# Graph network layer on one core: the first nodes and node numbers of the sums' one-hot matrices kept in PSUM

## The chip, the core and the metric

The kernel runs on one core of a Trainium2 chip. A core has TensorE (matrix products, which are written to PSUM), VectorE (DVE) and ScalarE (ACT) for elementwise work, GpSimd (POOL), which here issues the gathers, SyncE (SP), which issues the plain DMAs, and 16 DMA engines. SBUF is the working memory and PSUM the memory of 8 banks that the products land in; both have 128 partitions. The metric is the device time of one execution in microseconds (us); a kernel's time is the median over its runs.

## What is computed

The input is 6250 nodes with 512 features each and 100,000 edges (src, dst), sorted by dst. Cut to what matters:

```python
norm = -dinv[src] * dinv[dst]            # dinv = 1/sqrt(out-degree), 0 where there is none
def prop(h):                             # weighted sum over the incoming edges of each node
    return segment_sum(h[src] * norm[:, None], dst, num_segments=6250)
def conv(h, W0, W1, b):
    return h @ W0 + prop(h) @ W1 + b

h = maximum(layernorm(x), 0)
h = conv(h, W1_0, W1_1, b1)              # layer 1
h = layer_norm(h, gamma, beta)
h = where(h >= 0, h, 0.01 * h)
out = x + conv(h, W2_0, W2_1, b2)        # layer 2
```

All is in fp32. The heavy part is `prop`: for each of the 100,000 edges a row of 512 floats is fetched by its src and added to the row of its dst, once in each of the two layers.

## The kernel before

**Setup.** The kernel loads the edge list and x, counts the out-degrees with one-hot matmuls, takes the layer norm's statistics, and writes a table `tab` of rows already scaled by dinv, from which the first layer gathers. The edges are cut into NC = 782 chunks of 128, one edge on each partition. Transposed by TensorE, the chunks' source nodes become columns of `sidx`, and their destination nodes (plus one) columns of `dlx`; both stay in SBUF.

**Units and groups of the sums.** Three chunks (STEP) make a unit. A unit's sums cover a span of Q = 32 successive nodes, which begins at the node of the unit's first edge; four units (NQ) make a group and fill the 128 partitions of one PSUM tile. There are NS = 66 groups in a layer. The first node of every unit is found in the setup: the matmul of line 320 puts the last row of selected columns of `dlx` on all 128 partitions, in the PSUM tile `first_ps` of 265 columns, and line 321 copies that into `first` in SBUF.

**Gathers.** `gather_to` (line 379) issues one indirect DMA per chunk on GpSimd (line 382): 128 rows of 2 KB, picked by a column of `sidx`, into one of the 57 `places` in SBUF. Each layer has 782; the first 60 of layer 1 read x itself and 16 of those are issued early, on line 212. A place is used again when the matmuls of an earlier group have read it.

**Sums.** `sums(g)` (line 461) makes the one-hot matrices on VectorE and the sums on TensorE. Line 465 adds 1 to 32 to each of the group's four first nodes and so writes `node`, 128x128, a tile with two buffers. Line 474 compares the destination nodes of the group's chunks (`dlx`, read with broadcasts) with `node`, and so writes `sel`, 128x512, also with two buffers: a 1 stands where an edge of a partition belongs to a node of the span. Line 480 multiplies the 32 columns of `sel` of a chunk and a unit with the gathered rows; four chunks (SPAN) go into each unit, up to 16 products in a group, all into one `ps`. Line 483 copies `ps` to SBUF as `agg`.

**Blocks.** The nodes are also cut into 49 blocks of 128. When the groups that can hold a block's nodes are summed, `turn` transposes the block's own rows (`own`), and `place` moves its sums from the groups' spans to the block's rows by further one-hot products (`there`, line 493; matmul, line 496). `dense` multiplies both with the weights (line 458), and `finish` adds the bias and, in layer 1, takes layer norm, scales and stores the rows into the second layer's table `tab[1]` and into `h_tab`; in layer 2 it adds x and stores the result.

**Order.** TensorE, GpSimd and SyncE keep the order in which the program is written (a manual schedule); for VectorE and ScalarE a scheduler orders instructions by readiness and places the semaphores. In each group GpSimd is given the next 12 gathers first, then come the blocks that are due, the sums, and the dense products. In layer 1 there are also, in the opening, the tables that are still to be scaled (`make_table`, lines 393 to 397) and the look-up of scales for the rows gathered straight from x (`find` and `look_up`, lines 403 to 434). The second layer's first gather waits for the last row stored into `tab[1]`.

**PSUM.** In the loops the pool `main_ps` holds `ps`, `hT_ps` and `u_ps` with two buffers each and `aT_ps` with one: seven of the eight banks.

Of the kernel before, what the change touches and what calls it, by code (L numbers as in the profile page):

```python
# [8 lines left out]
F32 = mybir.dt.float32  # L9
# [10 lines left out]
P = 128  # L20
# [4 lines left out]
Q = 32  # L25
NQ = P // Q
# [13 lines left out]
def gnn_kernel(  # L40
# [33 lines left out]
    nc = tc.nc  # L74
    N, D = x.shape
# [10 lines left out]
    NS = -(-NU // NQ)  # L86
# [10 lines left out]
    tab = [dram.tile([n, D], F32, name=f"tab{i}") for i, n in enumerate((NB * P, N))]  # L97
    h_tab = dram.tile([N, D], F32, name="h_tab")
    ndinv_d = dram.tile([NB * P], F32, name="ndinv_d")

    ident = const.tile([P, P], F32, name="ident")
    iota_r = const.tile([P, P], F32, name="iota_r")
    ones = const.tile([P, P], F32, name="ones")
    eps = const.tile([P, 1], F32, name="eps")
# [5 lines left out]
    dlx = const.tile([P, 1 + STEP * NQ * NS + 1], F32, name="dlx")  # L110
    first = const.tile([P, NQ * NS + 1], F32, name="first")
    node_of = const.tile([P, NS], F32, name="node_of")
    minus = const.tile([P, 1], F32, name="minus")
# [5 lines left out]
    sidx = const.tile([P, NG * P], I32, name="sidx")  # L119
    w_sb = [const.tile([P, KD, D], F32, name=f"w{i}") for i in range(2)]  # L120
# [9 lines left out]
    stay = ExitStack()  # L130
# [2 lines left out]
    order = list(range(NB, NB + RE)) + list(range(w_at))  # L133
    w_late = places[:, w_at:NB, :].rearrange("p (i k) d -> p i k d", i=2)

    edges = ctx.enter_context(ExitStack())
    ep = edges.enter_context(tc.tile_pool(name="edges", bufs=1))
    src_i = ep.tile([EP, EJ], I32, name="src_i")
# [24 lines left out]
    while i < NB:  # L163
        n = min(NB - i, (2, 6, 8)[len(groups)] if len(groups) < 3 else 7)
# [37 lines left out]
    with tc.tile_pool(name="turn", bufs=1) as wp, tc.tile_pool(  # L202
        name="turn_ps", bufs=2, space=bass.MemoryType.PSUM
# [7 lines left out]
    for t in range(RE):  # L211
        nc.gpsimd.indirect_dma_start(
            out=places[:, order[t], :], out_offset=None, in_=x,
# [7 lines left out]
    for (i0, n), t in zip(groups, xs):  # L221
        n = min(n, NB - LAST - i0)
# [13 lines left out]
    with tc.tile_pool(name="deg", bufs=1) as dp, tc.tile_pool(name="onehot", bufs=2) as ohp, tc.tile_pool(  # L236
        name="deg_ps", bufs=1, space=bass.MemoryType.PSUM
# [37 lines left out]
    with tc.tile_pool(name="fold", bufs=1) as dp, tc.tile_pool(  # L275
        name="fold_ps", bufs=1, space=bass.MemoryType.PSUM
# [27 lines left out]
    with tc.tile_pool(name="turn", bufs=1) as wp, tc.tile_pool(  # L304
        name="turn_ps", bufs=1, space=bass.MemoryType.PSUM
    ) as wps:
        f = wp.tile([P, NG, P], F32, name="f")
        nc.vector.tensor_scalar_add(f, chunks[1], 1.0)
        dl_ps = wps.tile([P, NG * P], F32, name="dl_ps")
        for g in range(NG):  # L310
            nc.tensor.transpose(dl_ps[:, g * P : (g + 1) * P], f[:, g, :], ident)
        nc.scalar.activation(dlx[:, 1 : 1 + NC], dl_ps[:, :NC], AF.Copy)
        down = wp.tile([P, NG, P - 1], F32, name="down")
        nc.vector.tensor_tensor(down, f[:, :, 1:], f[:, :, : P - 1], op=OP.is_lt)
        nc.vector.tensor_reduce(unsorted, down.rearrange("p g e -> p (g e)"), AX.X, OP.add)


        last = ident[:, P - 1 : P]
        first_ps = wps.tile([P, NQ * NS + 1], F32, name="first_ps")
        nc.tensor.matmul(first_ps, last.to_broadcast([P, P]), dlx[:, 0 : STEP * NQ * NS + 1 : STEP], start=True, stop=True)  # L320
        nc.vector.tensor_copy(first, first_ps)
        row_ps = wps.tile([P, 2, NS], F32, name="row_ps")
        for k in range(2):
            for q in range(NQ):
                at = STEP * (q + k)
                nc.tensor.matmul(row_ps[q * Q : (q + 1) * Q, k, :], last.to_broadcast([P, Q]),
                                 dlx[:, at : at + STEP * NQ * (NS - 1) + 1 : STEP * NQ], start=True, stop=True)
        p_i = ep.tile([P, 1], I32, name="p_i")
        p_j = ep.tile([P, 1], F32, name="p_j")
        held = ep.tile([P, NS], F32, name="held")  # L330
        nc.vector.tensor_copy(p_i, p_id)
        nc.vector.tensor_single_scalar(p_i, p_i, Q - 1, op=OP.bitwise_and)
        nc.vector.tensor_copy(p_j, p_i)
        nc.vector.tensor_scalar(node_of, row_ps[:, 0, :], p_j, 1.0, op0=OP.add, op1=OP.add)
        nc.vector.tensor_tensor(held, row_ps[:, 1, :], node_of, op=OP.is_ge)
        nc.vector.tensor_mul(node_of, node_of, held)
        nc.vector.tensor_scalar_mul(minus, last, -1.0)
        rows_ps = wps.tile([NB, P], F32, name="rows_ps")
        nc.tensor.transpose(rows_ps, ndinv, ident)
        rows_sb = ep.tile([NB, P], F32, name="rows_sb")  # L340
        nc.scalar.activation(rows_sb, rows_ps, AF.Copy)
        nc.sync.dma_start(ndinv_d.rearrange("(b p) -> b p", p=P), rows_sb)

    edges.close()
    unseen = const.tile([1, 1], I32, name="unseen")
    usual_path(tc, locals())
    stay.close()
    n_unseen = nc.values_load(unseen[0:1, 0:1], min_val=0, max_val=1,
# [5 lines left out]

def usual_path(tc, have):
    nc = tc.nc
    (x, out, tab, h_tab, ndinv_d, sidx, dlx, iota_r, w_sb, W2_1, W2_0, w_late, ident, eps, ones, first, node_of, minus,
     unsorted, ln, dinv, sdinv, bias1, bias2, gam, bet, unseen, N, E, D, NB, NC, NU, NS, KD, rows, places, order,
     groups, xs, sc, pick, src_lo, src_hi, p_id, dup) = (
        have[n] for n in ("x out tab h_tab ndinv_d sidx dlx iota_r w_sb W2_1 W2_0 w_late ident eps ones first node_of "  # L360
                          "minus unsorted ln dinv sdinv bias1 bias2 gam bet unseen N E D NB NC NU NS KD rows places "
                          "order groups xs sc pick src_lo src_hi p_id dup").split())
    AHEAD = 2
# [5 lines left out]
    with ExitStack() as es:  # L369
        pool = es.enter_context(tc.tile_pool(name="main", bufs=2))  # L370
# [5 lines left out]
        def zr(t):  # L376
            return places[:, order[t % R], :]
# [83 lines left out]
        def sums(g):  # L461

            n = min(NQ, NU - NQ * g)
            node = pool.tile([P, NQ, Q], F32, name="node")
            nc.vector.tensor_tensor(node[:, :n, :], first[:, NQ * g : NQ * g + n, None].to_broadcast([P, n, Q]),
                                    iota_r[:, None, 1 : Q + 1].to_broadcast([P, n, Q]), op=OP.add)
            sel = pool.tile([P, NQ, SPAN, Q], F32, name="sel")
            chunk = [range(STEP * (NQ * g + q), min(STEP * (NQ * g + q) + SPAN, NC)) for q in range(n)]
            same = n if len(chunk[-1]) == SPAN else 1
            for q in range(0, n, same):  # L470
                w = len(chunk[q])
                of = dlx[:, 1 + chunk[q][0] : 2 + chunk[q][0]]
                of = bass.AP(tensor=of.tensor, offset=of.offset, ap=[of.ap[0], [STEP, same], [1, w], [0, Q]])
                nc.vector.tensor_tensor(sel[:, q : q + same, :w, :], of,  # L474
                                        node[:, q : q + same, None, :].to_broadcast([P, same, w, Q]), op=OP.is_equal)
            ps = psum.tile([P, D], F32, name="ps")
            for s in range(SPAN):
                for q in range(n):
                    if s < len(chunk[q]):
                        nc.tensor.matmul(ps[q * Q : (q + 1) * Q, :], sel[:, q, s, :], zr(chunk[q][s]), start=(s == 0),  # L480
                                         stop=(s == len(chunk[q]) - 1))
            agg[g] = pool.tile([P, D], F32, name="agg", bufs=4)
            nc.scalar.activation(agg[g][: n * Q], ps[: n * Q], AF.Copy)  # L483
# [134 lines left out]
        for layer in range(2):  # L618
# [5 lines left out]
            for g in range(NS):  # L624
# [13 lines left out]
                while inside[i].stop <= g:  # L638
                    due.append((i, turn(layer, i)))
                    i += 1  # L640
                sums(g)
                if layer == 0:
                    if g == 0:
# [344 lines left out]
```

## Time and profile before

| | us |
|---|---|
| median of 3 runs | 2149.52 |
| lowest and highest run | 2146.58, 2150.33 |
| the profiled execution | 2148.89 |
| its span, first to last instruction | 2146.7 |
| GpSimd busy, 1577 instructions | 1520.2 |
| TensorE busy with products | 1795.7 |
| VectorE busy | 674.8 |
| mean granted TensorE clock | 0.926 of full speed |

The profile is one execution, taken by the hardware profiler. Its lines are read like this. "L382 POOL DMA_INDIRECT places<-tab,sidx x1504 | 1444.5, 960 | 493.8 <-issue 315.8" says that line 382 of the kernel ran 1504 times on GpSimd, writing `places` from `tab` by the indices in `sidx`; 1444.5 us in all, 960 ns on average; before these instructions the engine was idle for 493.8 us, and most of that (315.8 us) ended with nothing that the profile shows ("issue"). PEld is TensorE's loading of weights, PE its products. In the row of 40 slices each digit is the busy share of a fortieth of the span, in tenths. A line of waits names the waiting engine, tile and line, then what it waited for, the sum in us, how often, and the longest one. A line of the timeline gives start and duration in us, engine, line, operation, the tiles written and read with their shapes, and in square brackets the idle time before it and what ended that.

### The profile page before, as it was taken

How to read it: one execution, taken by the hardware profiler on the slowest of the kernel's cores; microseconds unless marked ns; L12 is line 12 of the kernel's file. 1: busy time of each engine (PE TensorE's matmuls, PEld its weight loads, DVE VectorE, ACT ScalarE, POOL GpSimd, SP SyncE). 2: the span in 40 equal slices, each digit the busy share in tenths (PEclk: the TensorE clock that was granted, in tenths of full speed). 3: DMA queues.
4: the chain of work that ended last, by engine and by line, in shares of the span. 5: the costliest groups of instructions: out<-in, count | busy, mean ns of one | idle time of the engine just before them, and what ended most of it. 6: DMA issues, size and time to landing. Idle time of an engine off the chain costs nothing.

```text
span 2146.7 us, 23527 instructions
## 1 busy us (share of the span) xinstructions
PE 1795.7 (84%) x8843; PEld 794.7 (37%) x8843; DVE 674.8 (31%) x1341; ACT 382.7 (18%) x694; POOL 1520.2 (71%) x1577
## 2 busy tenths in 40 slices
PE   5669888988879888988876888889888888889888
PEld 4534333333334333433331333334333333334333
DVE  8974323333334233333330212212212212211211
ACT  7774212111112122111110000000000000000000
POOL 5067777777777777777727777777777777777772
PEclk9779999999989999999997989999999999999989
DMA  9298888788788888788837788888878888877883
GB/s 368 82 354 264 247 254 254 242 250 255 243 286 249 253 255 250 240 255 244 254 121 229 243 251 256 255 251 245 256 243 255 243 251 257 256 248 247 245 252 117
DMA packets 198945, 527.05 MB, mean 246 GB/s; under 512 B 31864, under 2 KB 46019, under 8 KB 198822
## 3 DMA queue, kind: packets, MB, share of 16 engines
q0 software_dynamic: 125120, 410.09, 62.4%
q1 hardware_dynamic: 73702, 115.36, 15.5%
q8 instruction: 71, 1.16, 0.2%
q14 instruction: 52, 0.43, 0.1%
HBM read 474.06 MB, written 51.27 MB: 245 GB/s over the span
## 4 chain that ended last, share of the span: by engine, by line
PE 48%; DMA 29%; POOL 9%; issue 8%; DVE 5%; ACT 0%; POOLq 0%; SPq 0%; ACTq 0%; DVEq 0%
DMA places<-tab,sidx 28%; PE u_ps L458 25%; PE ps L480 15%; POOL places L382 9%; PE aT_ps L496 5%; PE hT_ps L451 1%; DVE hi L252 1%; DVE lo L252 1%; DVE places L393 0%; PE both_ps L258 0%; DMA places<-in_x_dram,sidx 0%; DVE places L394 0%; PE u_ps L422 0%; PE hT_ps L422 0%; DVE both L428 0%
## 5 line engine op out<-in xcount | busy, mean ns | idle before, releaser
L382 POOL DMA_INDIRECT places<-tab,sidx x1504 | 1444.5, 960 | 493.8 <-issue 315.8
L480 PE MATMUL ps<-places,sel 128*32 128x512 f32 x4168 | 732.4, 666 | 280.7 <-DMA places<-tab,sidx 268.1
L480 PEld LDWEIGHTS ps<-places,sel 128*32 128x32 f32 x4168 | 141.8, 117 | 781.0 <-DMA places<-tab,sidx 591.3
L474 DVE TENSOR_TENSOR sel<-dlx,node 128x512 f32<-128x512 f32 x132 | 90.9, 688 | 750.0 <-PE ps L480 750.0
L496 PE MATMUL aT_ps<-there,agg 128*128 128x128 f32 (+2 forms) x2080 | 253.8, 278 | 1.4 <-ACT agg L483 1.4
L496 PEld LDWEIGHTS aT_ps<-there,agg 128*128 128x128 f32 (+1 forms) x2080 | 246.1, 196 | 4.2 <-ACT agg L483 3.2
L483 ACT ACTIVATE agg<-ps 128x512 f32<-128x512 f32 x132 | 78.8, 597 | 918.9 <-PE ps L480 918.9
L458 PE MATMUL u_ps<-places,hT 128*128 128x512 f32 (+1 forms) x392 | 185.8, 618 | 0.7 <-ACT hT L453 0.7
L458 PE MATMUL u_ps<-w,hT 128*128 128x512 f32 (+1 forms) x392 | 181.1, 605 | 0.7 <-ACT hT L453 0.7
L458 PE MATMUL u_ps<-places,aT 128*128 128x512 f32 (+1 forms) x392 | 178.0, 597 | 0.7 <-DVE aT L548 0.7
L458 PE MATMUL u_ps<-w,aT 128*128 128x512 f32 (+1 forms) x392 | 176.3, 592 | 0.7 <-DVE aT L548 0.7
L506 DVE TENSOR_TENSOR u_ps<-u_ps,bias 128x512 f32<-128x512 f32 x48 | 33.6, 700 | 294.9 <-PE u_ps L458 294.9
L511 DVE TENSOR_TENSOR u_ps<-u_ps,bias 128x512 f32<-128x512 f32 (+1 forms) x49 | 34.3, 700 | 284.3 <-PE u_ps L458 284.3
L453 ACT ACTIVATE hT<-hT_ps 128x512 f32<-128x512 f32 (+1 forms) x98 | 58.3, 595 | 349.6 <-PE hT_ps L451 348.2
L458 PEld LDWEIGHTS u_ps<-places,hT 128*128 128x128 f32 (+1 forms) x392 | 72.3, 195 | 117.3 <-issue 116.5
L458 PEld LDWEIGHTS u_ps<-w,hT 128*128 128x128 f32 (+1 forms) x392 | 70.3, 189 | 109.0 <-issue 106.5
L458 PEld LDWEIGHTS u_ps<-places,aT 128*128 128x128 f32 (+1 forms) x392 | 74.8, 191 | 95.4 <-issue 94.6
L458 PEld LDWEIGHTS u_ps<-w,aT 128*128 128x128 f32 (+1 forms) x392 | 74.3, 190 | 94.3 <-issue 93.4
L382 POOL DMA_INDIRECT places<-in_x_dram,sidx x44 | 45.0, 1024 | 86.8 <-ACT places L396 57.7
L448 ACT ACTIVATE h<-h,ln 128x512 f32<-128x512 f32 (+1 forms) x49 | 39.7, 813 | 283.3 <-DMA h<-in_x_dram 283.3
L493 DVE TENSOR_SCALAR there<-iota_r,node_of 128x128 f32<-128x128 f32 x260 | 76.6, 295 | 38.7 <-PE aT_ps L496 38.6
L548 DVE TENSOR_TENSOR aT<-aT_ps,to 128x512 f32<-128x512 f32 (+1 forms) x98 | 67.1, 685 | 39.4 <-PE aT_ps L496 37.9
(128 smaller groups left out, 942.7 us busy)
## 6 DMA issues: line engine op xcount, KB each, us to landing
places<-tab,sidx POOLq DMA_INDIRECT x1504
h<-in_x_dram SPq DMA_DIRECT2D x48, 256.0 KB
tab<-t SPq DMA_DIRECT2D x48, 256.0 KB
h_tab<-g SPq DMA_DIRECT2D x48, 256.0 KB
h<-h_tab SPq DMA_DIRECT2D x48, 256.0 KB
xt<-in_x_dram SPq DMA_DIRECT2D x48, 256.0 KB
out_dram<-t SPq DMA_DIRECT2D x48, 256.0 KB
places<-in_x_dram SPq DMA_DIRECT2D x4, 1792.0 KB
```

The source lines that it names most:

```text
L252: nc.vector.tensor_tensor(t, s[:, g * 2 * GJ : (g + 1) * 2 * GJ].rearrange("p (j s) -> p j s", s=2)[:, :, None, :] .to_broadcast([EP, GJ, ...
L382: nc.gpsimd.indirect_dma_start(out=zr(t), out_offset=None, in_=x if layer == 0 and t < RAW else tab[layer], in_offset=bass.IndirectOffsetO ...
L448: nc.scalar.activation(h[:r], h[:r], AF.Relu, bias=ln[:r, 1, i : i + 1], scale=ln[:r, 0, i : i + 1])
L453: nc.scalar.activation(hT[:, :, :r], ps[:, :, :r], AF.Copy)
L458: nc.tensor.matmul(u_ps[:r], hT[:, kc, :r], w[:, kc, :], start=(start and kc == 0), stop=(not start and kc == KD - 1))
L474: nc.vector.tensor_tensor(sel[:, q : q + same, :w, :], of, node[:, q : q + same, None, :].to_broadcast([P, same, w, Q]), op=OP.is_equal)
L480: nc.tensor.matmul(ps[q * Q : (q + 1) * Q, :], sel[:, q, s, :], zr(chunk[q][s]), start=(s == 0), stop=(s == len(chunk[q]) - 1))
L483: nc.scalar.activation(agg[g][: n * Q], ps[: n * Q], AF.Copy)
L493: nc.vector.tensor_scalar(there[:m, :r], iota_r[:m, :r], node_of[:m, g : g + 1], -(1.0 + i * P), op0=OP.subtract, op1=OP.is_equal)
L496: nc.tensor.matmul(placed[i][:, kc, :r], agg[g][:m, kc * P : (kc + 1) * P], there[:m, :r], start=(g == inside[i][0] and kc == 0), stop=(g ...
L511: nc.vector.tensor_add(v, v, bias1[:r])
L548: nc.vector.tensor_tensor(aT[:, :, :r], placed.pop(i)[:, :, :r], to.pop(i)[:, None, :r].to_broadcast([P, KD, r]), op=OP.mult)
```

## The change

The first nodes of the units no longer live in a tile of the setup's PSUM pool, but in a PSUM bank of their own, `nodes_ps`, which stays through both layers; the copy into `first` in SBUF is kept, since the final check reads it. The group's node numbers `node` are no longer an SBUF tile with two buffers, but the last 128 columns of the same bank, written anew for each group. So line 465 reads the first nodes from PSUM and writes PSUM, and line 474 reads `dlx` from SBUF and `node` from PSUM. No instruction is added or left out. `nodes_ps` takes the bank that `main_ps` leaves free.

```diff
@@ gnn_kernel
     w_late = places[:, w_at:NB, :].rearrange("p (i k) d -> p i k d", i=2)
 
+    nodes_ps = stay.enter_context(tc.tile_pool(name="nodes_ps", bufs=1, space=bass.MemoryType.PSUM)).tile(
+        [P, D], F32, name="nodes_ps")
+    assert NQ * NS + 1 <= D - P
     edges = ctx.enter_context(ExitStack())
...
         last = ident[:, P - 1 : P]
-        first_ps = wps.tile([P, NQ * NS + 1], F32, name="first_ps")
+        first_ps = nodes_ps[:, : NQ * NS + 1]
         nc.tensor.matmul(first_ps, last.to_broadcast([P, P]), dlx[:, 0 : STEP * NQ * NS + 1 : STEP], start=True, stop=True)
         nc.vector.tensor_copy(first, first_ps)
@@ usual_path: nodes_ps is handed over; then in sums(g)
             n = min(NQ, NU - NQ * g)
-            node = pool.tile([P, NQ, Q], F32, name="node")
-            nc.vector.tensor_tensor(node[:, :n, :], first[:, NQ * g : NQ * g + n, None].to_broadcast([P, n, Q]),
+
+            node = nodes_ps[:, D - P :].rearrange("p (q e) -> p q e", q=NQ)
+            nc.vector.tensor_tensor(node[:, :n, :], nodes_ps[:, NQ * g : NQ * g + n, None].to_broadcast([P, n, Q]),
                                     iota_r[:, None, 1 : Q + 1].to_broadcast([P, n, Q]), op=OP.add)
             sel = pool.tile([P, NQ, SPAN, Q], F32, name="sel")
```

More of the change, by code (lines that the diff above doesn't have):

```diff
@@ L356, in usual_path @@
     nc = tc.nc
-    (x, out, tab, h_tab, ndinv_d, sidx, dlx, iota_r, w_sb, W2_1, W2_0, w_late, ident, eps, ones, first, node_of, minus,
+    (x, out, tab, h_tab, ndinv_d, sidx, dlx, iota_r, w_sb, W2_1, W2_0, w_late, ident, eps, ones, first, nodes_ps, node_of, minus,
      unsorted, ln, dinv, sdinv, bias1, bias2, gam, bet, unseen, N, E, D, NB, NC, NU, NS, KD, rows, places, order,
      groups, xs, sc, pick, src_lo, src_hi, p_id, dup) = (
-        have[n] for n in ("x out tab h_tab ndinv_d sidx dlx iota_r w_sb W2_1 W2_0 w_late ident eps ones first node_of "
+        have[n] for n in ("x out tab h_tab ndinv_d sidx dlx iota_r w_sb W2_1 W2_0 w_late ident eps ones first nodes_ps node_of "
                           "minus unsorted ln dinv sdinv bias1 bias2 gam bet unseen N E D NB NC NU NS KD rows places "
```

## The prediction

> **What bounds the kernel now.** I read first the busy line, then the GpSimd row of the 40 slices, then the groups, then the waits of GpSimd and of the matmul engine, and last the timeline around single gathers.
>
> ```profile
> PE 1795.7 (84%) x8843; PEld 794.7 (37%) x8843; DVE 674.8 (31%) x1341; ACT 382.7 (18%) x694; POOL 1520.2 (71%) x1577
> POOL 5067777777777777777727777777777777777772
> ...
> L382 POOL DMA_INDIRECT places<-tab,sidx x1504 | 1444.5, 960 | 493.8 <-issue 315.8
> L474 DVE TENSOR_TENSOR sel<-dlx,node 128x512 f32<-128x512 f32 x132 | 90.9, 688 | 750.0 <-PE ps L480 750.0
> ```
>
> TensorE has the largest busy share, yet it is not what sets the pace. GpSimd's row is a flat 7 from the fourth slice to the end with one dip in the middle: a gather takes 0.95 us, and the next starts 0.30 us after it. A flat 7 is therefore an engine that always has its next gather ready, at 1.254 us a gather. The waits say the same from both sides:
>
> ```profile
> POOL places L382 <- issue: 320.7, 1052, 0.3
> POOL places L382 <- DMA tab<-t: 35.1, 1, 35.1
> POOL places L382 <- PE ps L480: 30.3, 98, 0.8
> ...
> PE ps L480 <- DMA places<-tab,sidx: 268.1, 198, 14.0
> PE ps L480 <- DVE sel L474: 10.0, 2, 8.1
> ```
>
> The last column is the longest single wait. GpSimd's waits for a freed place (PE ps) are the ordinary 0.3 us step between gathers; one is 0.8 us. The one real stop is the 35.1 us between the layers, when the second layer's first gather waits for the table that the first has finished. The matmuls wait 268.1 us for rows that have not landed, spread over both layers: in every full 100 us from 200 to 2100 TensorE sits idle 7.8 to 34 us. They wait for sel only twice, in the opening. So from about 126 us to the last gather at 2109.7 us time is the number of gathers times their pitch, plus the 35.1 us stop, plus whatever lengthens single gathers.
>
> Something does lengthen them. The gathers' median is 0.949 us, the mean 0.960, the longest 1.46. Two places in the timeline, Vector rows and GpSimd rows:
>
> ```profile
> 865.83 0.69 DVE L474 TENSOR_TENSOR sel<-dlx,node 128x512 f32<-128x512 f32 x1 [13.84 <-PE ps L480]
> 865.95 1.40 POOL L382 DMA_INDIRECT places<-tab,sidx  x1 [0.30 <-PE ps L480]
> 867.65 0.95 POOL L382 DMA_INDIRECT places<-tab,sidx  x1 [0.30 <-issue]
> ...
> 842.72 0.76 DVE L521 SCALAR_TENSOR_TENSOR u_ps<-u_ps,rs,bet 128x512 f32<-128x512 f32 x1
> 843.11 0.95 POOL L382 DMA_INDIRECT places<-tab,sidx  x1 [0.30 <-issue]
> ```
>
> The comparison L474 started 0.12 us before the gather at 865.95 and ended 0.57 us after the gather's start; the gather took 1.40 us, 0.45 too much. At 843.11 L521, with its data in PSUM, lay across a gather's start in the same way, and the gather took its 0.95. Over the whole trace the pattern is exact: where L474 runs from before a gather's start to more than 0.13 us after it, the gather is longer than 0.949 us by (end of L474 - start of gather - 0.13 us). From 126 us on, L474 lies so (0.15 us or more past the start) across 67 gathers and lengthens 61; L465, which also reads two SBUF tiles (first and iota_r), 7 of 11. Instructions that read one operand from PSUM and at most one wide operand from SBUF (L428, L506, L507, L511, L514, L519, L521, L525, L530, L548) lie so across 199 and lengthen none.
>
> **The change, part by part.** Nothing is added or removed: GpSimd and ScalarE have the same instructions in the same order, TensorE and VectorE the same number.
>
> *The lock on the gathers.* L474 reads dlx from SBUF and node from PSUM; L465 reads first from PSUM and iota_r from SBUF. Each has one SBUF input left. Summing each lengthened gather's excess over 0.949 us by the instruction whose end it follows: L474 10.70 us in layer 1 (36 gathers) and 7.00 us in layer 2 (25); L465 0.43 + 0.16 us and 0.25 us (8). Together 18.5 us. The page's rows check the size: 1444.5 - 1504 x 0.949 = 17.2 us for the gathers from tab, where 18.1 of my 18.5 us lie (the rest of the difference is gathers of 0.942 to 0.948). It is also what chance would give. An L474 of 0.693 us that starts at a random point of a 1.254 us pitch hits if it starts in the 0.563 us that end at the gather's start, with a mean excess of 0.28 us: 0.45 x 0.28 x 132 = 16.7 us.
>
> [...] I take 18.5 us; the other end is 0.
>
> *What stays locked.* L393 and L394 (2.6 us of excess before 145 us) and L425 (0.5 us) are untouched. L493 lengthened 4 gathers, 0.18 us in all. Its position relative to the gathers shifts; at random, 257 of 0.28 us would cost 257 x 0.12 x 0.075 = 2.3 us. Ends: 0 to 2.1 us more than now; I take 0.5, near the row, since its instructions follow the same TensorE work as before.
>
> *Duration of the two Vector instructions.* No row has L474's new pair (first input SBUF, second PSUM). [...] The nearest rows say none: L548, PSUM and SBUF to SBUF at the same size, takes 0.685, L507 0.691 against L474's 0.688; L506 and L511, which read and write one PSUM bank as L465 will, 0.700. I take 0.00 to 0.01 us each. Either way it costs no end time: VectorE is busy 31%, and sel is made a group ahead (two buffers, written when the sums two groups back are done), so some 15 us of other matmuls cover it. [...]
>
> *One buffer for node in place of two.* node of the next group must now follow sel of this one. In steady order it did already (at 866.56 L465 follows L474 at once). In the opening a few instructions change places: before, two L465 stand together ahead of the third L474; now each L465 follows its L474, so one node of 0.29 us moves. Behind it on VectorE is that L474, and TensorE waits for it. That is the only place where TensorE waits for sel (10.0 us), and GpSimd already runs ahead there: 0 to 0.3 us, taken as 0.
>
> *The PSUM bank.* The loops' seven banks and this one fill PSUM; the setup matmul L320 and copy L321 stay, one writing elsewhere. Cost 0; bounds -0.3 to +0.5 us, if some setup tile waits one matmul group for a shared bank.
>
> *What is late next.* Gathers land some 2.9 us after their issue ends, the same at the start and the end of a layer, so the DMA engines are not backed up at 81% busy; 1% more rate is absorbed. TensorE's slack, 7.8 us or more in each 100 us, stands against 0 to 1.6 us of savings in the same stretches, so it keeps up. The 35.1 us stop and the some 36 us after the last gather are chains of TensorE and Vector work that keep their length.
>
> **Sum.** 18.5 - 0.5 = 18.0 us off. The profiled execution took 2148.9 us (span 2146.7 and 2.2 around it): 2130.9. The median of the runs, 2149.5, is 0.6 above that execution, so I forecast 2131.5 us, 0.84% less.
>
> **The rivals.**
> - *Given back in part.* TensorE, or the chain at the layers' ends, takes over where blocks follow closely (a group with a block holds some 14.4 us of matmuls in a 15.05 us group), or L493 begins to hit. For: a margin of 0.6 us in those groups. Against: the idle time in every stretch. Half given back: 2140.
> - *No change.* The lock is not from two SBUF inputs but from something L474 keeps (dlx from SBUF as the first input, or the write to SBUF). For: no row has an SBUF first input beside a PSUM one. Against: L548 writes the same shape to SBUF across 40 gather starts without effect. 2149.5.
> - *Slower.* VectorE's single node buffer makes sel late: L465 queued behind an L474 that waits for the sums, TensorE stops at L480, and then the places come free late for GpSimd. Its place is every group, its point the 15 us by which sel is ahead; each us past it costs 132 us. An L474 of 0.76 us (the longest now) and an L465 of 0.36 are far below. Only if the PSUM reads took several us each would it decide; 2 us lost in a tenth of the groups gives 2149.5 - 18 + 26 = 2158.
>
> **How the numbers follow.** Full gain 0.82, in part 0.08, no change 0.05, slower 0.05. The likeliest gives 2131.5, its own range 2127 to 2137: the 18.5 us whole with a run at the low end of the three shown (2.9 below the median) up to L493 at random and 3 us at the layers' ends. For 8 in 10 with the partly lost cases, 2127 to 2141. What a measurement here can tell is about 0.2%, 4.3 us. Faster takes the first two cases, 0.90; same 0.05; slower 0.05.
>
> **What would show it.** Right: the gathers' mean falls from 0.960 to about 0.951 with the same 0.30 us step, no gather after 150 us over about 1.1 us, the longest ones beside L493; L474 and L465 within 0.02 us of now; the waits of GpSimd unchanged, the stop still about 35 us. Wrong: gathers still ending 0.82 us after an L474 does; GpSimd waiting for PE ps by more than a few us (TensorE bound); TensorE waiting for sel in mid-run.

## The result, and the profile after

The changed kernel takes 2127.65 us (median of 6 runs, 2126.33 to 2129.85). The kernel before, run beside it, takes 2145.54 us (median of 6, three of which are the runs shown above). The ratio is 0.9911, 95% interval 0.9898 to 0.9924: 19 us less by the ratio, 17.9 by the two medians. The forecast was 18.0 us less and 2131.5 us, its own range 2127 to 2137. The saving came as forecast; the absolute time came out 3.85 us under the forecast, at the lower edge of the range. The term that was off is the time from which the saving was taken, not the saving.

The page of the changed kernel (profiled execution 2129.0 us; its line numbers are 3 or 4 higher, so that L382, L474 and L493 of before are L385, L478 and L497):

```profile
span 2127.2 us, 23561 instructions
...
PE 1786.6 (84%) x8843; PEld 793.0 (37%) x8843; DVE 678.2 (32%) x1341; ACT 382.0 (18%) x694; POOL 1496.7 (70%) x1577
...
POOL 5057777777777777777727777777777777777772
...
L385 POOL DMA_INDIRECT places<-tab,sidx x1504 | 1422.6, 946 | 492.9 <-issue 313.8
L478 DVE TENSOR_TENSOR sel<-dlx,nodes_ps 128x512 f32<-128x512 f32 x132 | 89.8, 680 | 726.5 <-PE ps L484 726.4
```

GpSimd is busy 23.5 us less (1520.2 to 1496.7) and the span is 19.5 us shorter; its idle time before the gathers is the same (493.8 and 492.9), and its row is the same flat 7. VectorE is busy 3.4 us more. So the time left the gathers. The waits of GpSimd, and the two waits of TensorE that were to be watched, in the same columns as before:

```profile
POOL places L385 <- issue: 318.9, 1047, 0.3
...
POOL places L385 <- DMA tab<-t: 35.0, 1, 35.0
POOL places L385 <- PE ps L484: 21.0, 69, 0.3
...
PE ps L484 <- DMA places<-tab,sidx: 256.0, 174, 14.3
...
PE ps L484 <- DVE sel L478: 10.1, 2, 8.2
```

No wait took the place of the lock: GpSimd never waits longer than its step of 0.3 us for a place that the sums free, the stop between the layers kept its 35 us, TensorE still waits 256 us for rows, and for sel only the same two times in the opening.

Two views of the changed kernel's trace. The first is the row of its gathers from `tab`, with the shortest, median and longest duration in ns and the first and last start in us. The others show one comparison that lies across a gather's start:

```profile
L385 POOL DMA_INDIRECT places<-tab,sidx x1504: 942/946/1062, 174.1 to 2088.4; - x188
...
899.29 0.69 DVE L478 TENSOR_TENSOR sel<-dlx,nodes_ps 128x512 f32<-128x512 f32 x1 [4.70 <-PE ps L484]
...
899.53 0.95 POOL L385 DMA_INDIRECT places<-tab,sidx  x1 [0.30 <-issue]
```

The longest gather from tab is 1.06 us where it was 1.46. At 899.53 the comparison began 0.24 us ahead of the gather and ended 0.45 us into it; in the first trace of before the 11 comparisons that ended 0.43 to 0.47 us into a gather cost it 0.30 to 0.34 us, here it cost nothing. Over the trace the comparison lies across 69 gather starts (0.15 us or more past the start, from 125 us on) and lengthens none; the addition L469 lies across 10 and lengthens none.

### The profile page after: what moved, and what is told of

Same layout as the page of the kernel before. It is cut to its first block, busy times and chain, and to the rows that moved or that the text cites. A ratio compares the mean times of both kernels' runs of the same rounds, so it can differ in the third digit from the quotient of the medians.

```text
span 2127.2 us, 23561 instructions
## 1 busy us (share of the span) xinstructions
PE 1786.6 (84%) x8843; PEld 793.0 (37%) x8843; DVE 678.2 (32%) x1341; ACT 382.0 (18%) x694; POOL 1496.7 (70%) x1577
## 3 DMA queue, kind: packets, MB, share of 16 engines
q8 instruction: 71, 1.16, 0.2%
## 4 chain that ended last, share of the span: by engine, by line
PE 35%; DMA 32%; POOL 15%; issue 12%; DVE 4%; ACT 1%; POOLq 0%; SPq 0%; ACTq 0%; DVEq 0%
DMA places<-tab,sidx 32%; PE u_ps L461 16%; POOL places L385 15%; PE ps L484 13%; PE aT_ps L500 4%; PE hT_ps L454 1%; DVE hi L255 1%; DVE lo L255 1%; PE both_ps L261 1%; PE hT_ps L425 0%; DVE places L396 0%; ACT places L436 0%; DVE places L397 0%; PE u_ps L425 0%; DMA src_c<-in_src_dram 0%
## 5 line engine op out<-in xcount | busy, mean ns | idle before, releaser
L385 POOL DMA_INDIRECT places<-tab,sidx x1504 | 1422.6, 946 | 492.9 <-issue 313.8
L478 DVE TENSOR_TENSOR sel<-dlx,nodes_ps 128x512 f32<-128x512 f32 x132 | 89.8, 680 | 726.5 <-PE ps L484 726.4
L385 POOL DMA_INDIRECT places<-in_x_dram,sidx x44 | 43.5, 989 | 89.8 <-ACT places L399 58.8
L497 DVE TENSOR_SCALAR there<-iota_r,node_of 128x128 f32<-128x128 f32 x260 | 79.7, 307 | 43.3 <-PE aT_ps L500 41.4
```

What stands on the lines that cost most here:

```text
L385: nc.gpsimd.indirect_dma_start(out=zr(t), out_offset=None, in_=x if layer == 0 and t < RAW else tab[layer], in_offset=bass.IndirectOffsetO ...
L478: nc.vector.tensor_tensor(sel[:, q : q + same, :w, :], of, node[:, q : q + same, None, :].to_broadcast([P, same, w, Q]), op=OP.is_equal)
L497: nc.vector.tensor_scalar(there[:m, :r], iota_r[:m, :r], node_of[:m, g : g + 1], -(1.0 + i * P), op0=OP.subtract, op1=OP.is_equal)
```

## The experiments

Two theories stood against each other. *Lock:* a Vector instruction with two SBUF inputs that is running when a gather starts holds the gather up until it ends, and GpSimd's pace is the kernel's. (A gather that is held up is called hit.) *Rivals:* the time on VectorE counts, or where things lie in PSUM, or the gathers as such became shorter (their median was 949 ns in the first profile of before and 946 in that of after). In what follows "lengthened" means longer than 0.965 us, the excess is counted over the mean of the others in the same trace, and all is from 130 us on, after the opening.

### The kernel before again, and the changed one beside it

No edit. Both were profiled on the same chip.

> The kernel before, unchanged, profiled on the same chip as the runs beside it. Two profiles of different executions showed gathers of 0.949 us (before) and 0.946 us (after) in the median; 3 ns over 1548 gathers are 4.6 us. If that difference belongs to the execution or the chip and not to the change, this profile shows the same median as the changed kernel's profile of the same chip (within 1 ns), and the whole saving between the two spans is that of the lengthened gathers, some 17 to 18.5 us. If it belongs to the change, this one shows 0.949 again and the changed one 0.946. Ratio to itself 1.000 within 0.002. Lengthened gathers behind the comparison of 128x512: some 60, 16 to 19 us.

> The changed kernel, unchanged, on the same chip. Lock theory: ratio 0.9915 (18 us less) and no gather lengthened behind the two instructions that now read PSUM; the rival that the gathers as such became shorter: 0.9895 to 0.991, with the gathers' median 3 ns under that of the kernel before in the profile of this chip.

Measured: the kernel before 2149.7 us, ratio to its other runs 1.0005 (0.9995 to 1.0016); the changed one 2130.33 us, ratio 0.991 (0.9892 to 0.9927). The gathers of before, a comparison with the gather that it met, and then the gathers of the changed kernel:

```profile
L382 POOL DMA_INDIRECT places<-tab,sidx x1504: 942/949/1457, 172.8 to 2115.1; - x188
...
1251.32 0.69 DVE L474 TENSOR_TENSOR sel<-dlx,node 128x512 f32<-128x512 f32 x1 [3.69 <-PE ps L480]
...
1251.65 1.19 POOL L382 DMA_INDIRECT places<-tab,sidx  x1 [0.30 <-issue]
```

```profile
L385 POOL DMA_INDIRECT places<-tab,sidx x1504: 942/949/1023, 172.1 to 2093.1; - x188
```

Both have a median of 949 here: the changed kernel's 946 in its first profile was that execution's. So the gathers as such did not become shorter by the change; they have two levels (below). The ratio alone could not have said so: 0.991 is the edge of what that rival expected, and its interval holds the lock theory's 0.9915 as well. Lengthened: 90 gathers with 26.1 us before; 10 with 0.7 us after, none of them behind the two instructions that now read PSUM, which lay across 75 and 18 starts. The lock theory's 16 to 19 us behind the comparison was too low for this execution of before, which had 78 of them with 24.5 us and was the slowest of its ten runs (2156.69 us). How many gathers the comparison hits differs between executions of one kernel: 61 in the first trace of before, 78 in this one.

### The comparison alone

```diff
-            nc.vector.tensor_tensor(node[:, :n, :], nodes_ps[:, NQ * g : NQ * g + n, None].to_broadcast([P, n, Q]),
+            nc.vector.tensor_tensor(node[:, :n, :], first[:, NQ * g : NQ * g + n, None].to_broadcast([P, n, Q]),
```

This is an edit to the changed kernel: node stays in PSUM, the first nodes come from SBUF.

> The node numbers stand in PSUM and the comparison reads them there, as in the change; but the first nodes are read from SBUF, so the small addition (128x128) still has two SBUF inputs. Lock theory: of the 18.5 us the comparison's share, 17.7, is gained and the addition's 0.8 is not (between 0.3 and 3 us of lengthened gathers behind it, since its place relative to the gathers moves): ratio 0.9915 to 0.993. If both had to be in PSUM, or if it is the first nodes' place that counts, 0.998 to 1.000.

Measured: 2129.15 us, ratio 0.9906 (0.989 to 0.9921), 2.6 us of lengthened gathers. Behind the comparison none (65 starts), behind the addition with its two SBUF inputs 11 with 0.67 us. The gain is the comparison's; the addition's share is too small for the timing, but its gathers show it. The ratio lies just under the expected band, whose 0.9915 the interval holds.

### The addition alone

```diff
-            node = nodes_ps[:, D - P :].rearrange("p (q e) -> p q e", q=NQ)
+            node = pool.tile([P, NQ, Q], F32, name="node")
```

Again an edit to the changed kernel: the bank is reserved, the setup writes into it, the first nodes are read there, but node is a tile in SBUF.

> The first nodes are read from PSUM, but the node numbers are again a tile in SBUF with two buffers, so that the comparison has two SBUF inputs as before. Lock theory: only the addition's share is gained, 0.8 us: ratio 0.9996, between 0.998 and 1.001; some 60 gathers lengthened behind the comparison, 16 to 19 us. The rival that the reserved bank or the setup's other placement brings the gain: 0.991.

```profile
L385 POOL DMA_INDIRECT places<-tab,sidx x1504: 940/946/1452, 172.6 to 2106.5; - x188
L478 DVE TENSOR_TENSOR sel<-dlx,node 128x512 f32<-128x512 f32 x132 | 90.6, 686 | 745.8 <-PE ps L484 745.8
```

Measured: 2146.47 us, ratio 0.9999 (0.9987 to 1.0011). The comparison lengthened 66 gathers by 18.9 us, and the longest is 1.45 us again; the addition lay across 12 starts and lengthened none. The bank and the setup bring nothing that this measurement can tell (0.1%). This execution has the median of 946 with the lock in place, which again sets the two levels apart from the change.

### One more comparison, with two SBUF inputs or one

```diff
                 nc.vector.tensor_tensor(sel[:, q : q + same, :w, :], of,
                                         node[:, q : q + same, None, :].to_broadcast([P, same, w, Q]), op=OP.is_equal)
+                more = pool.tile([P, NQ, SPAN, Q], F32, name="more", bufs=1)
+                nc.vector.tensor_tensor(more[:, q : q + same, :w, :], of,
+                                        iota_r[:, None, None, :Q].to_broadcast([P, same, w, Q]), op=OP.is_equal)
```

The sister kernel has `node[:, q : q + same, None, :]`, in PSUM, in place of `iota_r[:, None, None, :Q]`, in SBUF.

> The changed kernel with one more comparison per group behind the first, 128x512, which reads dlx and node offsets 0 to 31, both from SBUF, and writes a tile that nobody reads: 132 instructions of some 0.69 us on VectorE. Lock theory: it hits as the kernel before did, 14 to 21 us of lengthened gathers, 0.999 to 1.002 of the kernel before. Rival, that VectorE's added time as such counts: the same as the variant whose added comparison reads PSUM. Rival, that GpSimd is not what sets the pace: gathers lengthened by 14 to 21 us, but the end moves by less than half of that.

> The changed kernel with one more comparison per group behind the first, 128x512, which reads dlx from SBUF and the node numbers from PSUM, and writes a tile that nobody reads: the same time on VectorE as its sister with two SBUF inputs. Lock theory: 0.991 to 0.993 of the kernel before, no gather lengthened by it; up to 2 us more for the later Vector work at the layers' ends. If the time on VectorE counts, 0.996 to 1.000.

With two SBUF inputs 2144.21 us, ratio 0.9983 (0.9972 to 0.9994); with one, 2126.61 us, 0.9906 (0.9891 to 0.9922). The added instructions and the gathers of the first, then of the second:

```profile
L481 DVE TENSOR_TENSOR more<-dlx,iota_r 128x512 f32<-128x512 f32 x132 | 90.0, 682 | 2.6
...
L385 POOL DMA_INDIRECT places<-tab,sidx x1504: 942/946/1410, 177.3 to 2102.5; - x188
```

```profile
L481 DVE TENSOR_TENSOR more<-dlx,nodes_ps 128x512 f32<-128x512 f32 x132 | 88.7, 672 | 0.0
...
L385 POOL DMA_INDIRECT places<-tab,sidx x1504: 940/946/1003, 171.6 to 2087.5; - x188
```

Both add Vector instructions of some 89 us. The one with an operand in PSUM costs nothing against the changed kernel; its sister gives back nearly all of the gain, 17.6 us between the two medians. Its added instruction lengthened 58 gathers by 12.9 us, a little under the 14 to 21 expected, and so its ratio lies just under the expected 0.999; the whole sum of gather times differs by 14.5 us between the two traces (1480.8 and 1466.4 us for the 1548 gathers from 96 us on) and the spans by 17.5, of which 2.4 lie after the last gather and 1.5 before the first. So it was not VectorE's time that counted here but where its operands lay, and what the gathers lost the end lost (14.5 us and 17.5).

### The comparison in four pieces

An edit to the kernel before, still with two SBUF inputs:

```diff
-            same = n if len(chunk[-1]) == SPAN else 1
+            same = 1
```

> The kernel before with the comparison cut into four of 128x128, one per unit, still with two SBUF inputs each: some 0.29 us each, and 0.9 to 1.2 us for the four. If the lock is let go between two instructions, a gather waits only for the one that it meets: a hit needs a start in the 0.16 us before a gather's, 0.13 x 0.08 us x 528 = 5.5 us in place of 17.7, ratio 0.993 to 0.996. If instructions that follow closely keep it (two additions in a row, of which the second began 0.08 us before the first ended, lengthened one gather by 0.35 us in the trace of before), the lock lasts some 0.95 us: 0.65 x 0.41 x 132 = 35 us, ratio 1.004 to 1.010.

```profile
L474 DVE TENSOR_TENSOR sel<-dlx,node x522: 226/284/360, 117.0 to 2088.0; 128x128 f32<-128x128 f32 x174
...
L382 POOL DMA_INDIRECT places<-tab,sidx x1504: 940/946/1194, 175.7 to 2095.5; - x188
```

Measured: 2135.35 us, ratio 0.9942 (0.9927 to 0.9956). The pieces lengthened 58 gathers by 4.7 us, 0.08 us each, where the whole comparison's cost 0.29 us each; 5.5 us and 0.08 were expected if the lock is let go between two instructions. For these it is, even where the next piece had begun some 0.08 us before the one that the gather met had ended. But one early gather was held much longer. First a usual hit, then that one (`x4` is four pieces in one row):

```profile
257.15 0.90 DVE L474 TENSOR_TENSOR sel<-dlx,node 128x128 f32<-128x128 f32 x4 [11.89 <-PE ps L480]
...
257.64 1.03 POOL L382 DMA_INDIRECT places<-tab,sidx  x1 [0.30 <-issue]
```

```profile
139.41 0.89 DVE L474 TENSOR_TENSOR sel<-dlx,node 128x128 f32<-128x128 f32 x4
140.22 0.48 DVE L465 TENSOR_TENSOR node<-first,iota_r 128x128 f32<-128x128 f32 x2
...
139.75 1.78 POOL L382 DMA_INDIRECT places<-in_x_dram,sidx  x1 [0.31 <-issue]
```

The gather at 257.64 met the third piece and ended 0.82 us after that piece, not after the fourth. The gather at 139.75 met the second piece and ended 0.82 us after the second of the two additions that followed the pieces closely: 1.78 us, 0.83 too much. At 193.60 a gather that met `there` (L493) was held through the addition behind it in the same way, 1.16 us. So the lock also passed through a row of instructions; of the pieces' 38 hits where another instruction with two SBUF inputs followed closely, it did so in one, and what decides it stays open. VectorE's busy time went up by 26.5 us (674.8 to 701.3) and the kernel became 11 us faster, without a byte moved to PSUM: what a collision cost was, with these exceptions, the rest of the instruction that it met.

## Why the prediction came out as it did

- **What bounds the kernel** (GpSimd's pitch): right. A change in the gathers' durations came out at the end in each pair, in one direction (the change: gathers 23.4 us less, span 19.5) and the other (the added comparison with two SBUF inputs: gathers 14.5 us more than with one, span 17.5).
- **The lock on the gathers, 18.5 us:** right in cause and size. In the first two profiles the lengthened gathers after 130 us went from 19.4 to 1.9 us, 17.5 less. As a number it was one draw, though: another execution of before lost 26.1 us, and behind a comparison of this size with two SBUF inputs four traces lost 12.9, 17.7, 18.9 and 24.5 us. That 18.0 us were forecast and the medians differ by 17.9 is in part luck. The estimate by chance, 16.7 us, lies among these too.
- **The two ends of the lock, 18.5 us or 0:** in the traces it went by the comparison's SBUF inputs. A comparison of 128x512 with both inputs in SBUF lengthened gathers in all four traces that have one (61, 78, 66 and 58 of them); with one input in PSUM the comparison lay across 69, 75 and 65 gather starts in three traces and lengthened none. At the end of 0 nothing would have been gained, and the medians differ by 17.9 us.
- **What stays locked, 0.5 us more:** right. L493 (L497 after) went from 5 gathers and 0.20 us to 11 and 0.47, 0.3 us more; the expected worst of 2.3 us didn't come.
- **Duration of the two instructions:** right, within the 0.01 us taken for each: the comparison went from a median of 693 to 687 ns, the addition from 291 to 299 ns. The rows of before had shown no added time for an operand in PSUM: L548 took 0.685 and L507 0.691 us, the comparison 0.688. And the added comparison with one SBUF input put 89 us more on VectorE and took 2126.61 us beside the changed kernel's 2127.65, so even more time there would have cost nothing.
- **One buffer, the bank, what is late next:** 0 as taken; TensorE's waits for sel are 10.0 and 10.1 us.
- **The rivals:** "no change" fell with the change's own trace (an SBUF first input beside a PSUM second one, 69 starts, none lengthened), "slower" with the waits, "given back in part" with TensorE's waits for rows, still 256 us.
- **The step that failed: the anchor, the sum's last step.** The prediction took its 18.0 us off the median of the three runs shown, 2149.5 us, and got 2131.5. Run beside the changed kernel, the kernel before had a median of 2145.54 us in six runs, these three among them, 4.0 us less; with it the same sum gives 2127.5, and 2127.65 was measured. Three runs could not carry that term: the medians of further sets of the same kernel are 2147.8 (23 runs), 2146.4 (17) and 2149.7 (10), and its single runs went from 2142.0 to 2156.7. What moves the median from set to set stays open.
- **The range, 2127 to 2137, held by luck.** The terms that are named for its low end (18.5 us whole, a run 2.9 us under the median) give 2128.1, and the measured time lies 0.5 below that.
- **The gathers' mean** was to fall from 0.960 to about 0.951. Its own 18.1 us over 1504 gathers make 0.948, and 0.946 was measured. The rest is the second level of the gathers, which the prediction put at nothing: 4.0 us between the two first profiles, and nothing in the one trace of before could tell of it.

The 19.5 us between the two first spans, as a sum: gathers from 96 us on 23.4 less (17.5 lengthened ones, 4.0 the other level, the rest in the opening); the first of them 1.1 later, 1.0 more in the stops, 1.8 more after the last one. The last of these is scatter of single executions, since in the second pair the tail went the other way, 38.5 to 36.8 us; the other two were not followed up.

## What to carry to other kernels

When GpSimd's gathers set the pace, look at their longest durations beside the median: a median of 0.95 and a maximum of 1.46 us pointed to the gain here, and laying each long one beside the Vector instruction that was running named its cause. What counted of the comparison was not the time that it takes of VectorE in all, but that it had two SBUF inputs and how long one instruction is; moving one operand to a free PSUM bank gained 0.9% here, cutting the instruction 0.6%. A forecast of an absolute time needs the scatter of more than three runs under it; the saving was predicted far better than the time.

## What the runs showed of the hardware

- **Who started first decided.** In the second trace of the kernel before, 78 of the 82 comparisons that ran on for 0.15 us or more past a gather's start lengthened the gather; they had started at least 0.056 us ahead of it. The other four had started at most 0.043 us ahead, ended 0.723 us after its start whatever their own start, and took up to 0.766 us instead of 0.693, while their gathers kept 0.945 to 0.949. These look as if VectorE waited for the gather.
- **What a hit costs.** From 200 us on, 401 of the 404 lengthened gathers in the nine traces end 0.81 to 0.84 us after the end of a Vector instruction with two SBUF inputs, whole or in pieces. The other three stand beside the small instructions of the kernel's own check of its numbers, at 634 to 638 us.
- **Two SBUF inputs were not the only form that held a gather.** Line 394 of `make_table` takes the larger of a tile in SBUF and 0, and writes the tile back; it has one SBUF input. In the first trace of before it ran on for 0.15 us or more past five gather starts, all before 134 us, and all five were lengthened. The last of them ended 0.82 us after line 394 did; why this form held it was not tried:

```profile
132.93 0.41 DVE L394 TENSOR_SCALAR places<-places 128x512 f32<-128x512 f32 x1
...
133.16 1.00 POOL L382 DMA_INDIRECT places<-in_x_dram,sidx  x1 [0.30 <-DVE is_hi L425]
```

- **Two levels of the gather.** The gathers that nothing lengthens average 947.8 to 948.1 ns in four profiles (before twice, after once, the comparison alone) and 945.4 to 945.6 in five (after once, the addition alone, both with the added comparison, the four pieces), for a whole execution each. Both levels appear on one chip, and for one kernel (the changed one). At 1540 gathers the 2.4 ns are 3.7 us. What sets the level wasn't tried and stays open.
